# A sparse graph-attention layer on one core: another order of the tiles, two products added on VectorE, an earlier request and another queue for the records

## The chip, the cores and the metric

The kernel runs on one core of a Trainium2 chip. A core has a matrix engine (TensorE, PE in the profile, with its weight loads shown apart as PEld), a vector engine (VectorE, DVE), a scalar engine (ScalarE, ACT), a general engine (GpSimd, POOL) and a sync engine (SyncE, SP) that only issues transfers. Each engine works through its own list of instructions in order and waits on semaphores for the others; DMA queues are fed from SP, ACT and POOL. The metric is the device time of one execution in microseconds, and the median of several executions is compared.

## The reference, cut to what matters

There are 4096 source nodes `x` and 4096 target nodes `h_target`, each of width 512, and an adjacency matrix of 4096 x 4096 integers with about 17 nonzero entries in a row. Eight heads have 64 columns each.

```python
hs = layer_norm(x, ln1);  ht = layer_norm(h_target, ln1)
q = (ht @ Wq + bq) / sqrt(64);  k = hs @ Wk + bk;  v = hs @ Wv + bv
logits = where(adj != 0, q @ k.T per head, -1e30)
ctx = softmax(logits) @ v
h = layer_norm(ht + ctx @ Wo + bo, ln2)
out = layernorm(x + h + gelu(h @ W1) @ W2)
```

W1 is 512 x 2048 and W2 is 2048 x 512. Everything is in 32-bit floats.

## The kernel before, in words

The kernel uses the sparsity. It makes, for every target row, a list of its neighbours, and gathers only those rows of k and v.

The first stage, to about 300 us, projects all sources to rows of k and v (a row of 1024 floats, kept in the DRAM tensor `kvd`), while the adjacency matrix is read in quarters of a row tile, and DVE takes the positions of the nonzero entries from them (`edges`). The targets are in two parts of 16 tiles of 128 rows. In each part the rows are sorted by their number of neighbours (`sort`), and a record is written for each row at its place in that order (`recs_d`): the number of neighbours, the row's index, its layer-norm factors and the first 24 neighbours. So each tile has rows of nearly equal degree and a fixed number of slots, `CAPS_A` for the first part and `CAPS_B` for the second: 39, 24, 23, 22, 20 and so on down to 11, and 38, 24, 23 and so on down to 12. The 603 slots in all are one gathered row of k and v for each of 128 targets. The lists of the first part and of five tiles of the second are made in the first stage, those of the rest beside the attention of the first part (`other_lists`).

In the second stage two streams are woven together at build time: attention over the tiles, and the feed-forward network over groups of tiles. `_order` puts the tiles in groups, almost always two, and so gives the order in which all of it runs. The function `_weave` merges the streams by due times: each generator yields a cost, and the one that is furthest behind goes next. A group of two tiles counts 60 units in attention (`cost`, shared out by slots) and 60 in the feed-forward stream, whatever its number of slots. A scheduler then gives each engine its final list, so instructions of one engine can change places.

Attention takes the slots of a tile in groups of up to three (`S = 3`, list `SG`). For a group:

- POOL gathers its slots into the ring `kv` by indirect DMA (`issue`, `gather`, L964). The ring has 17 places for the first part and 20 for the second. `request` issues four groups ahead, or five.
- DVE multiplies k by q (L1197) and sums over each head (L1201); ACT takes the exponential (L1205, L1214).
- DVE multiplies v by the weights (L1161), except for the third slot of a full group, which ACT does head by head (`by_scalar`, L1178 and L1181).
- PE transposes the slots and adds them up in PSUM, four transposes a slot (L1169). In the second part DVE adds the products of the first two slots before (L1165), so that PE transposes one less:

```python
if m > 1 and i >= NA:
    nc.vector.tensor_add(kv[:, 0, D:], kv[:, 0, D:], kv[:, 1, D:])
    slots.remove(1)
```

Before a tile's first group, `prefetch` loads its record (L978), two tiles ahead, into one of seven buffers, and `front` makes its q. It gathers the rows of `h_target` (into `tq`, one of three buffers), scales them on ACT (L990), transposes them on PE (L994, copied back by ACT at L997), multiplies by Wq (L1003) and adds the bias on DVE (L1008). The steps of `front` are spread by `yield`; each is made when `advance` is called, twice for a group of slots. A tile with more than 24 slots gets the rest of its list from `rest_of`, by a gather from `rest_d` and four DVE instructions. `finish` divides by the sums, multiplies by Wo (L1096), adds the normalized target by transposing `tq` (L1092), and makes the second layer norm and its transposes (L1122). `feed` multiplies by W1 (L1304), takes the gelu on ACT (L1307), multiplies by W2 (L1313), gathers x, and `end` normalizes and scatters the rows to the output by indirect DMA on POOL (L1281). The record of a tile is used last by that scatter, so its buffer is free when the scatter has landed.

Of the kernel before, what the change touches and what calls it, by code (L numbers as in the profile page):

```python
# [17 lines left out]
P = 128  # L18
# [360 lines left out]
RW = E0 + RE  # L379
# [5 lines left out]
def _order():  # L385


    n, m = len(CAPS_A), len(CAPS_B)
    a = [(k * P, c) for k, c in enumerate(CAPS_A)]
    b = [((n + k) * P, c) for k, c in enumerate(CAPS_B)]  # L390
    groups = [[a.pop()]]
    while len(a) > 1:
        groups.append([a.pop(), a.pop()])
    groups.append(a + [b.pop()])
    while len(b) > 1:
        groups.append([b.pop(0), b.pop()])
    return groups + [b]


def _weave(*streams):  # L400
# [43 lines left out]
def adj_resnorm_kernel(  # L444
# [33 lines left out]
    nc = tc.nc  # L478
# [14 lines left out]
    SEGS = [(s * WS, min(s * WS + WS, WQ)) for s in range(SQ)]  # L493
    SEG = NQ * SQ
    groups = _order()
    TILES = [t for g in groups for t in g]
    GROUPS = []
# [3 lines left out]
    NA, NBT = len(CAPS_A), len(CAPS_B)  # L501
# [11 lines left out]
    recs_d = [dram.tile([n * P, RW], I32, name=f"rec{i}") for i, (_, n) in enumerate(PARTS)]  # L513
# [19 lines left out]
    with tc.tile_pool(name="keep", bufs=1) as keep:  # L533
# [17 lines left out]
        with ExitStack() as late:  # L551
# [19 lines left out]
                                                                       b=2, s=SEG)  # L571
# [196 lines left out]
            def rest_of(i):  # L768


                keep_rest()
                rec = recs[i]
                gid = lp.tile([P, 2 * SEG, 8], F32, name="gid")
                flat = gid.rearrange("p s e -> p (s e)")
                gather(flat, rest_d, rec[:, TGT:TGT + 1])
                yield
                for c in range(E0 + RE, E0 + MAXE, 8):
                    nc.vector.match_replace(flat, rec[:, c - 8:c], flat, 0.0)
                    nc.vector.max(rec[:, c:c + 8], flat)
                has = lp.tile([P, MAXE], F32, name="ehas")  # L780
                num = lp.tile([P, 1], F32, name="num")
                nc.vector.tensor_scalar(has, rec[:, E0:E0 + MAXE], 0.0, 0.0, op0=ALU.is_gt,
                                        op1=ALU.add, accum_out=num)
                part = 1 if TILES[i][0] >= PARTS[1][0] * P else 0
                nc.vector.tensor_tensor(bad[:, 6 + part:7 + part], num, rec[:, DEG:DEG + 1],
                                        ALU.not_equal)
# [174 lines left out]
            recs, tqs, h2Ts, done, ready = {}, {}, {}, set(), []  # L961

            def gather(dst, table, idx):
                nc.gpsimd.indirect_dma_start(  # L964
                    out=dst, out_offset=None, in_=table[:, :],
                    in_offset=bass.IndirectOffsetOnAxis(ap=idx, axis=0))

            def prefetch(i):
                if i >= NT or i in recs:
                    return  # L970
                r0 = TILES[i][0]
                part = 1 if r0 >= PARTS[1][0] * P else 0
                assert part in done
                r0 -= PARTS[part][0] * P
                rec = sp.tile([P, E0 + MAXE], I32, name="rec", bufs=7)

                eng = nc.gpsimd if i < 2 else nc.sync
                eng.dma_start(rec[:, :RW], recs_d[part][r0:r0 + P, :])  # L978
                recs[i] = rec

            def front(i):


                rec = recs[i]
                tq = sp.tile([P, 2 * D], F32, name="tq", bufs=3)
                t = tq[:, :D]
                gather(t, h_target, rec[:, TGT:TGT + 1])
                yield
                m = rec[:, RST:RST + 2].bitcast(F32)
                nc.scalar.activation(t, t, AF.Identity, bias=m[:, 1:2], scale=m[:, 0:1])  # L990
                yield
                pt = ps.tile([P, KC, P], F32, name="t", bufs=2)
                for kc in range(KC):
                    nc.tensor.transpose(pt[:, kc, :], t[:, kc * P:(kc + 1) * P], ident)  # L994
                hT = tq[:, D:].rearrange("p (c t) -> p c t", c=KC)
                for kc in range(KC):
                    nc.scalar.activation(hT[:, kc, :], pt[:, kc, :], AF.Identity,  # L997
                                         bias=b1r[:, kc:kc + 1], scale=s1c[:, kc:kc + 1])
                yield
                yield  # L1000
                pq = ps.tile([P, D], F32, name="t", bufs=2)
                for kc in range(KC):
                    nc.tensor.matmul(pq, hT[:, kc, :], wq[:, kc, :], start=kc == 0,  # L1003
                                     stop=kc == KC - 1)
                yield
                yield
                yield
                nc.vector.scalar_tensor_tensor(tq[:, :D], pq, HD ** -0.5, bqr,  # L1008
                                               op0=ALU.mult, op1=ALU.add)
                tqs[i] = tq  # L1010


            SG = [(i, j0, min(S, cap - j0)) for i, (_, cap) in enumerate(TILES)
                  for j0 in range(0, cap, S)]
            kvs, rests, fronts = {}, {}, {}
            place = [0]
            for i, _, n in SG:
                if place[-1] + n > RING[i >= NA]:
                    place[-1] = 0
                place.append(place[-1] + n)  # L1020
            first_b = next(k for k, (i, _, _) in enumerate(SG) if i >= NA)
            issued = [0]

            def step(gens, i):

                if i in gens and next(gens[i], StopIteration) is StopIteration:
                    del gens[i]

            def request(k):
# [3 lines left out]
                while issued[0] <= min(k + ahead, len(SG) - 1):  # L1033
# [3 lines left out]
                        assert not mine & set(range(place[m], place[m] + SG[m][2]))  # L1037
                    issued[0] += 1

            def issue(k):  # L1040

                i, j0, n = SG[k]
                if j0 == 0:
                    prefetch(i + 2)
                    if i not in tqs:
                        fronts[i] = front(i)
                        step(fronts, i)
                    if TILES[i][1] > RE:
                        rests[i] = rest_of(i)
                        next(rests[i])  # L1050
                elif j0 + n > 12 and i in rests:
                    for _ in rests.pop(i):
                        pass
                kvs[k] = ring[:, place[k]:place[k] + n, :]
                for j in range(n):
                    gather(kvs[k][:, j, :], kvd[0:N + 1, :], recs[i][:, E0 + j0 + j:E0 + j0 + j + 1])

            def finish(i, p, cps, group, hs, mv):


                rec, tq, cap = recs[i], tqs.pop(i), TILES[i][1]
# [33 lines left out]
                for c in range(KC):  # L1095
                    nc.tensor.matmul(pa, ct[:, c, :], wo[:, c, :], start=False,  # L1096
                                     stop=c == KC - 1, skip_group_check=True)
                yield
                h = sp.tile([P, D], F32, name="h")
                nc.scalar.copy(h, pa)  # L1100
# [33 lines left out]
            def first_fronts():  # L1134

                for i in range(EARLY):
                    prefetch(i)
                for i in range(EARLY):
                    fronts[i] = front(i)
                while fronts:  # L1140
                    go_on()
                    yield 4.0

            def attention():
# [10 lines left out]
                def values(i, j0, n, kv, p, cps, after):  # L1155

                    m = n - 1 if n == S else n
                    v4 = kv[:, :m, D:].rearrange("p j (h d) -> p j h d", h=H)  # L1160
                    nc.vector.tensor_tensor(v4, v4, p[:, j0:j0 + m, :].unsqueeze(3)  # L1161
                                            .to_broadcast([P, m, H, HD]), ALU.mult)
                    slots = list(range(n))
                    if m > 1 and i >= NA:
                        nc.vector.tensor_add(kv[:, 0, D:], kv[:, 0, D:], kv[:, 1, D:])  # L1165
                        slots.remove(1)
                    for j in slots:
                        for c in range(KC):
                            nc.tensor.matmul(cps[:, c, :], kv[:, j, D + c * P:D + (c + 1) * P], ident,  # L1169
                                             is_transpose=True, start=j0 + j == 0 and c == 0,  # L1170
                                             stop=j0 + n == TILES[i][1] and j == slots[-1],
                                             skip_group_check=True)
                    if after is not None:
                        tails.append(after)
# [10 lines left out]
                k = 0  # L1185
                for group in GROUPS:
# [3 lines left out]
                    for i in group:  # L1190
                        cps = ps.tile([P, KC, P], F32, name="cps", bufs=2)
                        while k < len(SG) and SG[k][0] == i:
                            _, j0, n = SG[k]
# [162 lines left out]
                for g in gens:  # L1356
                    yield from g

            EARLY = 2
            WAIT = 40.0  # L1360
            AHEAD = 4
            UNIT = 60.0
# [102 lines left out]
```

## Time and profile before

| | |
|---|---|
| median of 5 runs | 1865.05 us (1858.57 to 1867.39) |
| the profiled execution | 1856.79 us, its span 1855.0 us |
| PE, PEld busy | 1691.5 us, 1104.4 us |
| DVE busy | 1429.4 us |
| ACT busy | 1212.0 us |
| POOL busy | 960.9 us |
| kv gathers on POOL (L964) | 603, 750.4 us, 1244 ns each |
| transposes of slots (L1169) | 2008, 261.8 us |
| adds of two products (L1165) | 101, 68.6 us |
| end of the eighth tile, of the tile with 39 slots, of the last tile (L1066) | 604, 1026, 1710 us |

Busy time is the time in which an engine had an instruction in work; it is no measure of whether it set the pace. The windows give it for a stretch of the span, and the waits tell which engine or transfer an idle engine was waiting for. The times of the L1066 instruction, one for each tile, tell where attention is. In a line of the timeline the numbers are the start, the length, and in square brackets the idle time before it and what ended that. The compared times are of whole executions, and the profiled one lies 8 us below their median.

### The profile page before, as it was taken

The numbers are of one execution on the slowest core, as the hardware profiler recorded it, in microseconds if no ns is written. First come the engines' busy times: TensorE is split into PE (matmuls) and PEld (weight loads), VectorE is DVE, ScalarE is ACT, GpSimd is POOL, SyncE is SP. The second block draws the span as 40 slices with busy tenths as digits, with TensorE's granted clock in tenths as the row PEclk, the third lists the DMA queues.
The fourth block names the chain that finished last, engine by engine and source line by source line (L and its number), as shares of the span: only waits on it lengthen the run. The fifth ranks groups of instructions, "written<-read, shape, count | busy, mean of one in ns | idle before, by whom it ended". The sixth has DMA issues, their size and how long they took to land. (4 is left out here: it accounts for less than half of the span.)

```text
span 1855.0 us, 22978 instructions
## 1 busy us (share of the span) xinstructions
PE 1691.5 (91%) x7030; PEld 1104.4 (60%) x7030; DVE 1429.4 (77%) x2596; ACT 1212.0 (65%) x3111; POOL 960.9 (52%) x804
## 2 busy tenths in 40 slices
PE   7989974697989989999999989899999999999995
PEld 3434432475656656767666666576676666656663
DVE  6989855999989838777968999788978697778000
ACT  5767634587877637676767776676868676756211
POOL 1000143845646577657567788776657566643101
PEclk9999987799999989999999999899999999999998
DMA  9999959988877548768788888778777776763000
GB/s 353 364 378 375 346 168 353 337 289 315 295 274 235 201 137 301 260 227 273 252 275 301 266 301 285 245 263 264 222 251 241 247 261 222 248 204 114 23 0 25
DMA packets 147757, 463.28 MB, mean 250 GB/s; under 512 B 24468, under 2 KB 29160, under 8 KB 147624
## 3 DMA queue, kind: packets, MB, share of 16 engines
q0 software_dynamic: 95696, 342.19, 54.3%
q1 hardware_dynamic: 44112, 96.44, 14.7%
q10 hardware_dynamic: 7816, 23.08, 3.3%
q8 instruction: 58, 0.95, 0.2%
q14 instruction: 75, 0.61, 0.1%
HBM read 430.76 MB, written 30.89 MB: 249 GB/s over the span
## 5 line engine op out<-in xcount | busy, mean ns | idle before, releaser
L964 POOL DMA_INDIRECT kv<-kvd,rec x603 | 750.4, 1244 | 406.1 <-PE cps L1169 161.0
L1313 PE MATMUL po<-w,gt 128*128 128x512 f32 x1024 | 470.0, 602 | 7.2 <-ACT gt L1307 7.2
L1304 PE MATMUL pf<-h2T,w 128*128 128x256 f32 (+1 forms) x2176 | 472.2, 371 | 1.7 <-issue 1.7
L1197 DVE TENSOR_TENSOR kv<-kv,tq 128x1536 f32<-128x1536 f32 (+2 forms) x211 | 352.0, 1676 | 111.1 <-DMA kv<-kvd,rec 96.4
L1304 PEld LDWEIGHTS pf<-h2T,w 128*128 128x128 f32 x2176 | 393.9, 193 | 68.6 <-issue 23.4
L1181 ACT ACTIVATE kv<-kv,pa 128x64 f32<-128x64 f32 x1520 | 391.4, 336 | 4.5
L1201 DVE TENSOR_REDUCE lg<-kv 128x24 f32<-128x1536 f32 (+2 forms) x211 | 350.4, 1667 | 6.7 <-ACT pa L1178 5.7
L1313 PEld LDWEIGHTS po<-w,gt 128*128 128x128 f32 x1024 | 190.6, 194 | 205.2 <-issue 196.5
L1169 PEld LDWEIGHTS cps<-ident,kv 128*128 128x128 f32 x2008 | 237.9, 144 | 108.9 <-issue 49.0
L1169 PE MATMUL cps<-ident,kv 128*128 128x128 f32 x2008 | 261.8, 278 | 42.7 <-DVE kv L1161 39.6
L1161 DVE TENSOR_TENSOR kv<-kv,p 128x1024 f32<-128x1024 f32 (+1 forms) x211 | 250.8, 1193 | 19.2 <-ACT p L1205 9.7
L687 POOL TENSOR_TENSOR n_rs<-n_ve,mhalf 128x2 f32<-128x2 f32 (+2 forms) x51 | 54.2, 1063 | 349.7 <-DVE n_ve L680 144.6
L728 ACT ACTIVATE kv<-kv 128x1024 uint8<-128x1024 int32 x128 | 134.7, 1053 | 78.2 <-DMA kv<-in_adj_dram 40.0
L929 PE MATMUL pq<-wk,h2T 128*128 128x512 f32 x256 | 126.7, 639 | 11.8 <-ACT h2T L914 5.6
L1307 ACT ACTIVATE gt<-pf 128x512 f32<-128x512 f32 x128 | 76.3, 596 | 91.7 <-PE pf L1304 84.0
L735 DVE MAX8 cand<-kv 128x8 uint16<-128x103 uint16 (+1 forms) x640 | 130.4, 252 | 1.4 <-issue 0.5
L1307 ACT ACT_TABLE_LOAD x99 | 127.0, 1283 | 1.6
L1205 ACT ACTIVATE p<-lg 128x24 f32<-128x24 f32 (+2 forms) x179 | 39.0, 218 | 134.6 <-DVE lg L1201 100.2
L1003 PE MATMUL t<-wq,tq 128*128 128x512 f32 x256 | 118.6, 606 | 8.9 <-ACT tq L997 8.9
L929 PE MATMUL pq<-wv,h2T 128*128 128x512 f32 x256 | 115.3, 593 | 0.8 <-ACT tq L931 0.8
L1096 PE MATMUL t<-wo,rb 128*128 128x512 f32 x256 | 115.5, 592 | 0.0
L990 ACT ACTIVATE tq<-tq,rec 128x512 f32<-128x512 f32 x32 | 26.0, 813 | 110.0 <-DMA tq<-in_L_gnn_h_target_dram,rec 109.8
(156 smaller groups left out, 1574.3 us busy)
## 6 DMA issues: line engine op xcount, KB each, us to landing
kv<-in_adj_dram SPq DMA_DIRECT2D x128, 512.0 KB
kvd<-tq ACTq DMA_DIRECT2D x24, 512.0 KB
kv<-kvd,rec POOLq DMA_INDIRECT x603
kv<-in_L_gnn_h_target_dram SPq DMA_DIRECT2D x32, 256.0 KB
kv<-in_x_dram SPq DMA_DIRECT2D x15, 512.0 KB
rest_d<-gid SPq DMA_DIRECT2D x32, 160.0 KB
w<-in_L_gnn_W_dram SPq DMA_DIRECT2D x4, 1024.0 KB
kvd<-kv ACTq DMA_DIRECT2D x8, 512.0 KB
```

The costliest lines, as they stand in the source:

```text
L728: nc.scalar.activation(sg, a, AF.Sign, accum_out=dpart[:, i, h:h + 1])
L735: nc.vector.max(cand[:, h * SQ + s, :], wd[:, w0:w1])
L929: nc.tensor.matmul(pkv, hT[:, kc, j * P:(j + 1) * P], w[:, kc, :], start=kc == 0, stop=kc == KC - 1)
L964: nc.gpsimd.indirect_dma_start(out=dst, out_offset=None, in_=table[:, :], in_offset=bass.IndirectOffsetOnAxis(ap=idx, axis=0))
L1161: nc.vector.tensor_tensor(v4, v4, p[:, j0:j0 + m, :].unsqueeze(3) .to_broadcast([P, m, H, HD]), ALU.mult)
L1169: nc.tensor.matmul(cps[:, c, :], kv[:, j, D + c * P:D + (c + 1) * P], ident, is_transpose=True, start=j0 + j == 0 and c == 0, stop=j0 + n ...
L1181: nc.scalar.mul(v, v, pa[:, hd:hd + 1])
L1197: nc.vector.tensor_tensor(kv[:, :n, :D], kv[:, :n, :D], tq[:, :D].unsqueeze(1).to_broadcast([P, n, D]), ALU.mult)
L1201: nc.vector.tensor_reduce(lg[:, :n, :], kv[:, :n, :D].rearrange("p j (h d) -> p j h d", h=H), AX.X, ALU.add)
L1304: nc.tensor.matmul(pf[:, k, :], w1[(f0 + k) // KC][:, kc, (f0 + k) % KC * P:((f0 + k) % KC + 1) * P], h2T[:, kc, :w], start=kc == 0, stop= ...
L1307: nc.scalar.activation(gt, pf, AF.Gelu_apprx_tanh)
L1313: nc.tensor.matmul(po[j], gt[:, k, j * P:(j + 1) * P], w2[(f0 + k) // KC][:, (f0 + k) % KC, :], start=False, stop=f0 + k == FC - 1, skip_g ...
```

## The change

There are four edits. The first changes `_order`: the heaviest tile of each part, with 39 and 38 slots, moves from the border between the parts to a place inside its part, each with a partner of 13 slots as its own group. In slots the order of groups is

- before: 11; 13+14; 15+15; 16+17; 17+18; 19+19; 20+22; 23+24; 39+12; 38+13; 24+14; 23+15; 22+15; 20+16; 19+17; 18+17; 18
- after: 11; 14+15; 15+16; 17+17; 18+19; 19+20; 13+39; 22+23; 24+12; 24+14; 23+15; 22+15; 38+13; 20+16; 19+17; 18+17; 18

The second lets DVE add the products of two slots from the ninth tile on, instead of from the seventeenth. The third begins `front` of a tile up to two groups of slots sooner, when its `tq` buffer has been read by PE for the last time in program order (`turned`); its further steps are put off by as many calls, and by two more in the second part. The fourth issues all record loads from POOL, where the first two were, instead of from SP.

```diff
 def _order():
     groups = [[a.pop()]]
+    top = [a.pop(), a.pop(0)]
     while len(a) > 1:
         groups.append([a.pop(), a.pop()])
+    groups.insert(-1, top)
     groups.append(a + [b.pop()])
+    top = [b.pop(0), b.pop()]
+    rest = []
     while len(b) > 1:
-        groups.append([b.pop(0), b.pop()])
-    return groups + [b]
+        rest.append([b.pop(0), b.pop()])
+    rest.insert(len(rest) // 2, top)
+    return groups + rest + [b]
...
-                eng = nc.gpsimd if i < 2 else nc.sync
-                eng.dma_start(rec[:, :RW], recs_d[part][r0:r0 + P, :])
+                nc.gpsimd.dma_start(rec[:, :RW], recs_d[part][r0:r0 + P, :])
...
-            def front(i):
+            def front(i, idle=0):
...
                 gather(t, h_target, rec[:, TGT:TGT + 1])
-                yield
+                for _ in range(1 + idle):
+                    yield
...
+            def begin(i, lead):
+                if i not in begun_fronts:
+                    begun_fronts.add(i)
+                    fronts[i] = front(i, 2 * lead + (2 if i > NA else 0))
+                    step(fronts, i)
+
             def issue(k):
+                for d in (1, 2):
+                    if k + d < len(SG) and SG[k + d][1] == 0 and SG[k + d][0] - 3 in turned:
+                        begin(SG[k + d][0], d)
                 i, j0, n = SG[k]
                 if j0 == 0:
                     prefetch(i + 2)
-                    if i not in tqs:
-                        fronts[i] = front(i)
-                        step(fronts, i)
+                    begin(i, 0)
...
                 for c in range(KC):
                     nc.tensor.matmul(pa, ct[:, c, :], wo[:, c, :], start=False,
                                      stop=c == KC - 1, skip_group_check=True)
+                turned.add(i)
...
-                    if m > 1 and i >= NA:
+                    if m > 1 and i >= NA - 8:
```

More of the change, by code (lines that the diff above doesn't have):

```diff
@@ L1010, in front @@
                 tqs[i] = tq
+            EARLY = 2
             SG = [(i, j0, min(S, cap - j0)) for i, (_, cap) in enumerate(TILES)
@@ L1020, in adj_resnorm_kernel @@
                 place.append(place[-1] + n)
+            begun_fronts, turned = set(range(EARLY)), set()
             first_b = next(k for k, (i, _, _) in enumerate(SG) if i >= NA)
@@ L1357, in chain @@
                     yield from g
-            EARLY = 2
             WAIT = 40.0
```

## The prediction, made before the changed kernel was run

> **What bounds the kernel now.** I read the page's busy shares and slices first, then windows cut at the ends of tiles, then groups of instructions, waits, and single stretches of the timeline.
>
> ```profile
> PE 1691.5 (91%) x7030; PEld 1104.4 (60%) x7030; DVE 1429.4 (77%) x2596; ACT 1212.0 (65%) x3111; POOL 960.9 (52%) x804
> ...
> PE   7989974697989989999999989899999999999995
> ...
> DVE  6989855999989838777968999788978697778000
> ```
>
> The second of these, the slices, matters more than the shares: from slice 16 (about 720 us) on PE is full almost everywhere and stays so to the end, 130 us after DVE has nothing left to do. In slices 8 to 13 it is DVE that is full.
>
> ```profile
> 350.00:600.00 250.00, 217.06 (x1016) 151.01 (x1015) 233.58 (x508) 193.46 (x491) 140.79 (x109) 0.94 0.81 281
> ...
> 600.00:720.00 120.00, 111.73 (x492) 75.58 (x491) 78.14 (x98) 66.96 (x181) 79.21 (x69) 0.96 0.61 204
> 720.00:1026.00 306.00, 298.31 (x1405) 211.25 (x1404) 249.05 (x242) 226.70 (x635) 199.04 (x171) 0.98 0.78 266
> 1026.00:1160.00 134.00, 125.76 (x567) 87.77 (x566) 125.55 (x131) 97.08 (x278) 106.68 (x78) 0.97 0.84 283
> 1160.00:1700.00 540.00, 519.25 (x2199) 350.24 (x2198) 443.74 (x474) 384.23 (x1039) 342.78 (x276) 0.98 0.72 238
> 1710.00:1838.00 128.00, 124.71 (x524) 83.10 (x522) 12.71 (x74) 23.99 (x46) 10.25 (x12) 1.00 0.05 15
> ```
>
> Columns after the length: busy PE, PEld, DVE, ACT, POOL. Four regimes: 350 to 600, DVE at 93% with the list work of part two beside attention; 720 to 1026, PE at 97% and DVE at 81%; 1026 to 1160, the tiles of 12, 38 and 13 slots, DVE and PE both at 94%; then PE at 96% and DVE at 82%. So 94% is the highest share that DVE reaches here in a mixed stretch, and PE work that goes between 604 and 1700 is worth its own time as long as DVE stays below that.
>
> ```profile
> POOL kv L964 <- PE cps L1169: 161.0, 86, 15.7
> ...
> ACT tq L990 <- DMA tq<-in_L_gnn_h_target_dram,rec: 109.8, 25, 10.7
> ...
> DVE kv L1197 <- DMA kv<-kvd,rec: 96.4, 34, 12.4
> ```
>
> POOL waits for PE to free the ring: PE is what the others wait for. ACT's wait for h is long, but of it only the L994 transposes (20.9 us, four times) reach PE.
>
> ```profile
> 497.73 1.53 PE L1169 MATMUL cps<-ident,kv 128*128 128x128 f32 x12 [1.05 <-DVE kv L1161]
> ...
> 1255.66 1.75 DVE L1197 TENSOR_TENSOR kv<-kv,tq 128x1536 f32<-128x1536 f32 x1
> 1257.33 0.68 DVE L1165 TENSOR_TENSOR kv<-kv 128x512 f32<-128x512 f32 x1
> 1257.93 1.74 DVE L1201 TENSOR_REDUCE lg<-kv 128x24 f32<-128x1536 f32 x1
> 1259.59 1.21 DVE L1161 TENSOR_TENSOR kv<-kv,p 128x1024 f32<-128x1024 f32 x1
> 1260.72 1.75 DVE L1197 TENSOR_TENSOR kv<-kv,tq 128x1536 f32<-128x1536 f32 x1
> ...
> 757.95 0.99 POOL L1281 DMA_INDIRECT out_dram<-xt,rec  x1 [0.30 <-ACT rb L1073]
> 761.86 0.98 POOL L964 DMA_INDIRECT xt<-in_x_dram,rec  x1 [2.92 <-DMA out_dram<-xt,rec]
> ...
> 265.13 1.17 POOL L978 DMA_DIRECT2D rec<-rec  x2 [1.77 <-issue]
> 271.53 1.01 POOL L964 DMA_INDIRECT tq<-in_L_gnn_h_target_dram,rec  x1 [5.24 <-DMA rec<-rec]
> ```
>
> Prices: twelve transposes in 1.53 us, the last taking 0.28, so one costs (1.53 - 0.28) / 11 = 0.114 us. On DVE, start to start, a group of three slots costs 1.67 (L1197) + 1.66 (L1201) + 1.13 (L1161) = 4.46 us, 1.49 a slot; the add L1165 makes it 5.06. A record load on POOL takes 0.6 us plus 0.3 of issue, and what needs it at once waits 5.24 us more; a gather behind an output scatter waits 2.9.
>
> **What the Trainium skill says.** "Perfetto Trace Analysis", Identifying the Most-Contended Engine, warns that matmul busy time is no measure of distance to roofline. Agreed, PEld is only 69% busy from 720 to 1026; I take PE as the bound because of who waits for whom. "SBUF — State Buffer", Practical consequences, says that a DVE instruction with two SBUF inputs contends with a GpSimd one that reads SBUF. The kv gathers of POOL take 0.94 us or about 2 us and 1.24 in the mean, which fits; 59 more adds of that kind can cost POOL up to 59 x 0.6 = 35 us, against 161 us that it waits for PE. "DMA: Bandwidth & Descriptors", Anatomy of one DMA — SWDGE, gives 2.0 us plus bytes/436e3, an estimate of 2.0 us for a 14.5 KB record load; the trace has 5.24 after issue, and that is used.
>
> **The change part by part.**
>
> *Adds.* They now apply to tiles 8 to 15: 19, 19, 20, 13, 39, 22, 23 and 24 slots, in which 59 groups have two or more DVE slots. PE loses 59 x 4 = 236 transposes: 236 x 0.114 = **-27 us**, all after 600 us, where PE is the bound. DVE gains 59 x 0.60 = 35 us. Does it fit? Tiles 8 to 15 ran from 604 to 1026 with PE 111.7 + 298.3 = 410 and DVE 78.1 + 249.0 = 327 us busy. Five slots leave this stretch (123 instead of 118 lie in the first eight tiles): PE 410 - 27 - 2 = 381, DVE 327 + 35 - 7 = 355. On average DVE is 93% of PE, so mostly hidden.
>
> *Order, first half.* Not on average but in one pair it does not fit: 13 + 39 slots on DVE is 17 x 5.06 + 1.8 + about 12 (the other instructions of two tiles, and the 39 slots' own list end) = 100 us, at 94% 106; PE has some 94 to 97 (a pair of feeds, projections and transposes about 78, slots 52 x 0.456 - 7.8). **+10 us** there, 0 if DVE's lead of a few groups covers it, +20 if the stalls also cost clock. Five slots moved in front of 604 us meet a full DVE: 5 x 1.49 = **+7**, and **-2** of PE after it.
>
> *Order, second half.* Before, 39 + 12 and 38 + 13 slots stand back to back, and PE idles 7.7 us (720 to 1026) and 8.2 us (1026 to 1160). With 24 + 12 after the first, and 38 + 13 in the midst of part two behind pairs that leave DVE 18% free, I take half of the 16 back: **-8** (0 to -16). Moved with the 39-slot tile go its 39 kv gathers, its h gather, its gather of list rests and its record load; all stay in POOL's order, the latter three now in one run behind two scatters.
>
> *h sooner.* In the changed program as built, POOL's order has the h gather about 4 to 5 slots before its tile in part two, instead of about 2; but ACT's order has the scaling L990 at five groups before the tile instead of three or four. The consumer moves as far as the request. I take **0** (-15 if the L994 waits go, +10 if ACT waits longer). Behind a waiting L990 stand the exponentials, the by-ACT products and the gelus; PE waits for those.
>
> *Record loads.* 30 leave SP, where they waited 907 us that cost nobody (only at 497 us did list loads stand behind one), and enter POOL: 30 x 0.9 = 27 us, against POOL's 161 + 62 us of waiting for the ring. They stand right behind the scatters whose landing they wait for, where the x gather waited already, and seven h gathers follow their own record with at most one gather between: up to 7 x 5 = 35 us of POOL standing still, with kv gathers behind. DVE sees it when its ring of five to six groups runs dry. **+5 us** taken, 0 to +40.
>
> Sum: -27 - 2 + 7 + 10 - 8 + 0 + 5 = **-15 us**. The profiled execution took 1856.8 us with a span of 1855.0, so 1841.8 and a span of 1840; it is 8 us below the median of the five runs, so I forecast 1865 - 15 = **1850 us**.
>
> **Rivals.**
>
> A, *the uneven pair is absorbed and the h waits go*. DVE enters the heavy pair with its ring full, PE's idle 16 us come back, and half of the L994 and L1079 waits of PE go (20.9 + 24.0, half 22, of which some 5 lie in those 16 already): -27 - 2 + 7 - 16 - 17 = -55, so 1810. For: the 97% of PE ahead of the pair. Against: the L990 order above.
>
> B, *DVE becomes the bound in tiles 8 to 15* (slower). DVE was idle 426 - 327 = 99 us in this stretch, and waits for kv, ACT and POOL rather than merely for PE. If that idle time is not squeezed, the stretch takes 355 + 99 = 454 instead of 426: +28, with +7 and -8 that is +27: 1892 us; half squeezed, 1867. It decides from the point where idle stays above 71 us. Against: idle was 6% in 1026 to 1160.
>
> C, *POOL's run at the end of each feed starves DVE*. Scatter, landing, record, landing, h, and only then kv: some 4 us more at a dozen places, half of it passed on, +24: 1865 - 20 + 24 = 1869.
>
> D, *nothing moves*: the adds are paid where PE's time is saved. 1865.
>
> **How the numbers follow.** Forecast 0.50 (own range 1838 to 1862), A 0.17, B 0.16, C 0.09, D 0.08. A measurement of this kernel can tell about 0.3%, 5.6 us, from no change. Faster: 0.50 x 0.9 + 0.17 + a little of C = 0.63; slower: most of B and C and the tail of the forecast, 0.23; the same 0.14. Leaving half of A's tail and the upper part of B out, the range is 1820 to 1877.
>
> **What would show it.** L1169 with 1772 matmuls and L1165 with 160; the stretch from 604 us to the end of the 24-slot tile shorter by 15 to 25 us, with DVE near 90% and PE still above 94%; PE waiting for DVE (cps on L1161 or L1165) by about 10 us in the 13 + 39 pair; the h waits of ACT about as long as before; the POOL wait on record landings new, 10 to 35 us, and DVE's wait for kv up by less than 30. It is wrong if DVE's share there stays near 81% and the stretch does not shorten (B), or if PE's waits on L994 vanish and the time falls below 1835 (A).

## The result, and the profile after

| | before | after |
|---|---|---|
| median | 1861.4 us (79 runs, 1846.65 to 1875.39) | 1855.52 us (42 runs, 1846.13 to 1861.33) |
| ratio of the times, with 95% interval | 1 | 0.9971 (0.9962 to 0.9980) |
| profiled execution, its span | 1856.79 us, 1855.0 us | 1854.99 us, 1853.2 us |
| start of the last output scatter | 1838.8 us | 1844.7 us |
| from that start to the end of the span | 16.2 us | 8.5 us |

The change saves 0.29% or about 6 us, where 15 us were forecast. The last two rows hold the surprise. In the profiled executions all of the work ends 6 us later than before; the gain lies behind the last scatter, where nothing is computed any more. The profiled execution of the kernel before was 4.6 us faster than its median, so between the medians the work ends about 2 us later.

From the page of the changed kernel, the busy shares, the slices of PE and DVE, and the groups of the transposes and of the adds:

```profile
PE 1672.7 (90%) x6794; PEld 1080.7 (58%) x6794; DVE 1459.8 (79%) x2655; ACT 1229.3 (66%) x3125; POOL 974.0 (53%) x834
...
PE   7989974597999789989899899998989999999997
...
DVE  6989854899899767889898787887889897988200
...
L1187 PE MATMUL cps<-ident,kv 128*128 128x128 f32 x1772 | 243.1, 283 | 69.7 <-DMA kv<-kvd,rec 24.8
...
L1183 DVE TENSOR_TENSOR kv<-kv 128x512 f32<-128x512 f32 x160 | 109.2, 683 | 0.5
```

236 transposes are gone and 59 adds have come, as worked out: PE is busy 19 us less, DVE 30 us more. But in slices 15 to 22 (counted from 0, about 695 to 1065 us), where PE had nines alone, there are now three eights. The windows, cut at the ends of the eighth tile (628 us), of the 24-slot tile (1029), of the 12-slot tile (1054) and of the last tile (1719), have busy PE, PEld, DVE, ACT and POOL after the length. The first is of the kernel before, from its eighth tile to the end of its 39-slot tile; the others are of the changed kernel:

```profile
604.00:1026.00 422.00, 406.05 (x1874) 283.25 (x1873) 323.19 (x327) 291.08 (x809) 274.90 (x237) 0.98 0.73 248
```

```profile
628.00:1029.00 401.00, 364.31 (x1555) 247.37 (x1554) 339.50 (x366) 283.58 (x771) 284.54 (x237) 0.96 0.76 250
...
1054.00:1719.00 665.00, 641.74 (x2743) 432.46 (x2742) 555.36 (x597) 487.54 (x1302) 424.67 (x357) 0.99 0.72 242
```

The stretch that got the adds has PE at 364.31 / 401 = 91% and DVE at 339.50 / 401 = 85%. Before, the same eight places in the order had PE at 406.05 / 422 = 96% and DVE at 77%. So PE's saved time has partly become PE's idle time, and DVE is not full either. After 1054 us PE is at 96.5%, much as before. The first number behind the five busy times is the share of PE's full clock that was granted: 0.98 before and 0.96 after in this stretch. The waits name what PE waits for (us in total, times, longest):

```profile
POOL kv L970 <- PE cps L1187: 137.0, 68, 11.6
...
ACT tq L996 <- DMA tq<-in_L_gnn_h_target_dram,rec: 121.7, 27, 10.7
...
DVE kv L1215 <- DMA kv<-kvd,rec: 32.1, 10, 12.3
...
PE cps L1187 <- DVE kv L1183: 23.8, 9, 10.1
...
POOL rec L983 <- DMA out_dram<-xt,rec: 22.2, 9, 4.5
...
PE t L1000 <- ACT tq L996: 16.0, 3, 9.0
```

The line of PE and the add (L1187 and L1183) is new: 23.8 us of PE's waits end with the add, and the list before had no such entry. POOL waits less for PE (137.0 us, before 161.0), DVE much less for its gathers (32.1, before 96.4), and POOL now 22.2 us for scatters to land before a record load. ACT's waits for h are a little longer, and PE's at the h transposes a little shorter (16.0, before 20.9). One of the nine cases, in DVE's and PE's lines of the timeline:

```profile
786.28 1.23 DVE L1179 TENSOR_TENSOR kv<-kv,p 128x1024 f32<-128x1024 f32 x1 [4.19 <-ACT p L1232]
791.68 1.76 DVE L1215 TENSOR_TENSOR kv<-kv,tq 128x1536 f32<-128x1536 f32 x1 [4.18 <-DMA kv<-kvd,rec]
793.36 0.68 DVE L1183 TENSOR_TENSOR kv<-kv 128x512 f32<-128x512 f32 x1
...
794.10 1.97 PE L1187 MATMUL cps<-ident,kv 128*128 128x128 f32 x8 [5.16 <-DVE kv L1183]
```

The products are ready at 787.5 us. The add needs nothing else, but on DVE's list the multiply of the next group (L1215) stands ahead of it, and that waits 4.18 us for its gather. DVE idles with the add ready behind it, and PE, out of other work since 788.9 us, waits 5.16 us; without the add it could have started on the products at once. Not every case is so pure. Eight of the nine waits, 22.0 us, lie in tiles 8 to 15, and only some 12 us of these passed after the product was ready; in the other 10 us the product itself was late. In the longest one, 10.1 us, the product was ready 2.3 us before PE began. Of the 160 adds only 19 directly follow their product on DVE; 41 have a multiply L1215 of another group between, and 47 a reduce L1219 (counted in the trace; the rest has other work between, or more than one instruction).

Last, the instructions of POOL's end-of-program line (shortest, median and longest of three drains in ns), first in the kernel before:

```profile
L1460 POOLq DRAIN  x3: 44/107/8158, 1846.1 to 1854.8; - x3
```

and in the changed kernel:

```profile
L1477 POOLq DRAIN  x3: 44/107/1952, 1850.4 to 1852.9; - x3
```

One drain of POOL takes 8.16 us before and 1.95 us after. That is 6.2 of the 7.7 us by which the end came closer to the last scatter.

### The profile page after: what moved, and what is told of

Read it like the earlier page. It is cut to its first block, busy times and chain, and to the rows that moved or that the text cites. A ratio compares the mean times of both kernels' runs of the same rounds, so it can differ in the third digit from the quotient of the medians.

```text
span 1853.2 us, 22478 instructions
## 1 busy us (share of the span) xinstructions
PE 1672.7 (90%) x6794; PEld 1080.7 (58%) x6794; DVE 1459.8 (79%) x2655; ACT 1229.3 (66%) x3125; POOL 974.0 (53%) x834
## 5 line engine op out<-in xcount | busy, mean ns | idle before, releaser
L970 POOL DMA_INDIRECT kv<-kvd,rec x603 | 750.1, 1244 | 409.1 <-PE cps L1187 137.0
L1331 PE MATMUL po<-w,gt 128*128 128x512 f32 x1024 | 464.4, 596 | 2.7 <-ACT gt L1325 2.5
L1215 DVE TENSOR_TENSOR kv<-kv,tq 128x1536 f32<-128x1536 f32 (+2 forms) x211 | 351.8, 1676 | 36.3 <-DMA kv<-kvd,rec 32.1
L1219 DVE TENSOR_REDUCE lg<-kv 128x24 f32<-128x1536 f32 (+2 forms) x211 | 350.3, 1667 | 0.2
L1187 PE MATMUL cps<-ident,kv 128*128 128x128 f32 x1772 | 243.1, 283 | 69.7 <-DMA kv<-kvd,rec 24.8
L1187 PEld LDWEIGHTS cps<-ident,kv 128*128 128x128 f32 x1772 | 215.9, 147 | 142.0 <-issue 50.4
L734 ACT ACTIVATE kv<-kv 128x1024 uint8<-128x1024 int32 x128 | 134.8, 1054 | 85.9 <-DMA kv<-in_adj_dram 50.6
L935 PE MATMUL pq<-wk,h2T 128*128 128x512 f32 x256 | 122.5, 622 | 8.9 <-ACT tq L937 5.8
L935 PE MATMUL pq<-wv,h2T 128*128 128x512 f32 x256 | 119.2, 610 | 7.0 <-ACT kv L937 6.7
L1183 DVE TENSOR_TENSOR kv<-kv 128x512 f32<-128x512 f32 x160 | 109.2, 683 | 0.5
```

The lines of the kernel that those rows point to most:

```text
L734: nc.scalar.activation(sg, a, AF.Sign, accum_out=dpart[:, i, h:h + 1])
L935: nc.tensor.matmul(pkv, hT[:, kc, j * P:(j + 1) * P], w[:, kc, :], start=kc == 0, stop=kc == KC - 1)
L970: nc.gpsimd.indirect_dma_start(out=dst, out_offset=None, in_=table[:, :], in_offset=bass.IndirectOffsetOnAxis(ap=idx, axis=0))
L1215: nc.vector.tensor_tensor(kv[:, :n, :D], kv[:, :n, :D], tq[:, :D].unsqueeze(1).to_broadcast([P, n, D]), ALU.mult)
L1219: nc.vector.tensor_reduce(lg[:, :n, :], kv[:, :n, :D].rearrange("p j (h d) -> p j h d", h=H), AX.X, ALU.add)
L1331: nc.tensor.matmul(po[j], gt[:, k, j * P:(j + 1) * P], w2[(f0 + k) // KC][:, (f0 + k) % KC, :], start=False, stop=f0 + k == FC - 1, skip_g ...
```

## The experiments

Each ratio is to the kernel before on the same chip, in five rounds, with its 95% interval; the groups of experiments ran on different chips. Line numbers shift a little between kernels; the operations are named. "Tail" is the time from the start of the last scatter to the end of the span. The expectations number their theories. Mine at first was 1 (the adds pay, the new order takes part of it back) with 4 (the effects add up); against it stood 2 (DVE is the bound), 3 (h or the records take it back), 5 and 7 (the adds pay only with the early h, or with it and the order) and 6 (PE waits for the add). Later ones are on the records and the drain (8 to 11), on why the adds return nothing (12: DVE has no time; 13: PE waits for the add itself) and on h (15: the distance from gather to scaling; 16: q is ready sooner).

### One edit alone, and three without one

Eight kernels: each edit alone on the kernel before, and each undone in the changed kernel. The switches are

```diff
# adds                                     # records
-  if m > 1 and i >= NA:                   -  eng = nc.gpsimd if i < 2 else nc.sync
+  if m > 1 and i >= NA - 8:               +  eng = nc.gpsimd
# order: the body of _order                # h: front's idle steps, begin, turned
```

> The kernel before with the second edit alone: DVE adds two products from the ninth tile on (here the tiles of 18, 19, 19, 20, 22, 23, 24 and 39 slots). Theory 1 (adds pay, the new order eats it): 10 to 25 us faster than before, 236 to 248 transposes fewer. Theory 2 (DVE becomes the bound in these tiles): within 5 us of before or slower, DVE over 94% busy there. Theory 3 (adds pay, the h request or the record loads eat it): 10 to 25 us faster, like theory 1.

> The kernel before with the first edit alone: the new order of tiles. Theory 1: 5 to 15 us slower (five more slots in front of the ninth tile, where DVE is full, and nothing regained in part two). Theory 2: 5 to 10 us faster, since the heavy pairs are apart. Theory 3: within 5 us of before.

> The kernel before with the third edit alone: h requested sooner. Theory 1 and 2: within 4 us of before, since the scaling on ACT moves with the request. Theory 3: 5 to 12 us slower, PE waiting longer before the q matmuls (L1009) for ACT.

> The kernel before with the fourth edit alone: all record loads in POOL's queue. Theory 1 and 2: within 4 us of before. Theory 3: 5 to 10 us slower, POOL waiting for landings of scatters and records at the end of each feed.

> The changed kernel without the second edit (adds from the seventeenth tile on, as before). Theory 4 (the effects add up; alone they were order +0.14%, adds +0.43%, h -0.65%, records +0.55%): 0.7% faster than before. Theory 5 (the adds pay only where the h request is early and the 39-slot tile stands apart from the 38-slot one): between 0.3% slower and 0.2% faster, so slower than the changed kernel.

> The changed kernel without the first edit (order of tiles as before). Theory 4: 0.4% faster than before. Theory 5: 0.2 to 0.8% slower, the adds making DVE the bound around the adjacent tiles of 39 and 38 slots.

> The changed kernel without the third edit (h requested as before). Theory 4: 0.35% slower than before. Theory 5: 0.5 to 1% slower, since the record loads on POOL delay the h gather, and PE waits for the scaling, at every tile.

> The changed kernel without the fourth edit (records on SP, as before). Theory 4: 0.85% faster than before, and so 0.55% faster than the changed kernel. Theory 5: 0.3 to 0.6% faster than before, the record loads on POOL costing less when h is requested early.

| edit | alone | undone in the changed kernel (0.9971) | so worth there |
|---|---|---|---|
| adds | 1.0043 (1.0026 to 1.0060) | 1.0011 (0.9996 to 1.0025) | -0.40% |
| order | 1.0014 (0.9996 to 1.0031) | 0.9977 (0.9958 to 0.9995) | -0.06% |
| h sooner | 0.9935 (0.9911 to 0.9959) | 0.9996 (0.9981 to 1.0012) | -0.25% |
| records on POOL | 1.0055 (1.0038 to 1.0073) | 0.9956 (0.9938 to 0.9973) | +0.15% |

The edit that was priced at nothing, h, is the only one that gains alone: 12 us. The adds, meant to carry the forecast with -27 us, cost 8 us alone. The records cost 10 us alone and 3 us in the changed kernel. The order is worth nothing that these intervals can tell from zero. Theories 1 and 3 expected the adds to gain alone, and no theory expected a gain from h. Theory 2 has the sign of the adds, but not its reason: DVE was busy for 83% of their stretch and not for over 94%. Theory 3 has the records. With the edits undone, adds and records came out as theory 5 had it, the order nearest to theory 4, and h as neither.

The effects do not add up: alone they sum to +0.47%, together they make -0.29%. In the changed kernel the adds do gain, 0.40%. There the records are loaded from POOL; with them on SP, and the new order and the early h in both, the adds gain nothing (0.9956 with them, 0.9947 without, the latter from the next section). Put the other way, the records on POOL cost 0.64% without the adds and 0.15% with them. Why the two go together is not shown.

The profile of the kernel with the adds alone has the wait on the add, too:

```profile
PE cps L1169 <- DVE kv L1165: 27.9, 14, 5.5
```

### Two edits

The adds or the order on top of the earlier h, to see whether they need it.

> The kernel before with the second and third edits: DVE adds from the ninth tile on, and h requested sooner. Theory 6 (the adds return nothing anywhere: PE waits for the add, L1165, about as long as the transposes would have taken; they looked good in the changed kernel only against its record loads): 0.5 to 0.9% faster than before, like the h edit alone at 0.65%. Theory 7 (the adds need the early h and bring their 25 us then): 1.2 to 1.8% faster.

> The kernel before with the first and third edits: new order and early h. Theory 6: 0.4 to 0.7% faster than before, the order being worth about nothing. Theory 7: 0.1% slower to 0.2% faster: without the adds the new order is only a load, as in the changed kernel without the adds (+0.11%).

Adds with h: 0.9950 (0.9933 to 0.9968); order with h: 0.9947 (0.9931 to 0.9962). Either is within 0.15% of h alone (0.9935), so the adds return nothing even there: theory 6 for both, and theory 7 is refuted. In the profile of adds with h PE's wait for the add is larger still. Of these 35.3 us, 22 lie in tiles 8 to 15, as with the adds alone (21) and in the changed kernel (22); the rest is of the second part:

```profile
PE cps L1182 <- DVE kv L1178: 35.3, 16, 5.7
```

### The cost and the gain of the adds, each alone

On top of the earlier h, two kernels for tiles 8 to 15. In the first, DVE makes the adds but writes them into the used-up k half of the slot, and PE transposes all slots as before: the cost without the gain. In the second, the second slot is neither added nor transposed: the gain without the cost.

```diff
 # cost alone
+    elif m > 1 and i >= NA - 8:
+        nc.vector.tensor_add(kv[:, 0, :D], kv[:, 0, D:], kv[:, 1, D:])
 # gain alone
+    elif m > 1 and i >= NA - 8:
+        slots.remove(1)
```

> The kernel before with the third edit, and in the ninth to sixteenth tile DVE adds the two products as in the second edit, but writes the sum over the used k of the first slot; PE still transposes every slot. So the adds are paid and nothing is saved. Theory 12 (capacity: DVE's own time comes back as PE's wait): 15 to 30 us slower than with the h edit alone, so 0.2 to 0.9% slower than before. Theory 13 (PE loses only because its transposes now wait for the add itself): at most 5 us slower than with the h edit alone, 0.4 to 0.65% faster than before.

> The kernel before with the third edit, and in the ninth to sixteenth tile the second slot of a group is neither added nor transposed: its product is left out of the sum. So PE's saving comes without DVE's cost. Theory 12: 15 to 27 us faster than with the h edit alone, 1.4 to 2.1% faster than before. Theory 14 (PE's time is not worth its length even there, since DVE, POOL and ACT hold the tiles up): less than 8 us faster than the h edit alone.

Cost alone: 0.9894 (0.9865 to 0.9923), not slower than h alone, as theory 13 had it. Gain alone: 0.9825 (0.9797 to 0.9852), some 20 us below h alone; so theory 14 is out, and PE's time is worth most of its length. The following table is worked out from the traces, for the stretch from the end of the eighth to that of the sixteenth tile. "Need" is PE's instructions at the shortest spacing seen for their width, 109, 215 and 429 ns for 128, 256 and 512 columns, and "lost" is the rest. "Idle" is the part of it in gaps of over 0.15 us, and the last column is the time in which PE was granted half of its clock.

| kernel, with h | stretch | PE need | PE lost | of it idle | idle until the add | at half clock |
|---|---|---|---|---|---|---|
| no adds here | 424 us | 398 | 26 | 17 | none | 14 |
| cost alone | 427 us | 400 | 28 | 18 | none | 14 |
| gain alone | 406 us | 375 | 32 | 22 | none | 17 |
| both | 434 us | 386 | 49 | 30 | 22 | 31 |

With both, the need falls by 12 us and not by 23 as with the gain alone, since more of the feed-forward work lies in the stretch; what counts is the time lost. It grows by 23 us: 13 are more idle time, and the other 10 go with PE's clock, at half for 31 us instead of 14. In the trace four of the five stretches at half clock begin in, or just behind, a wait of over 2 us for the add. So the waits seem to bring the lower clock; no run tests that by itself. Of the 22 us, some 16 passed after the product was ready. The table is of single executions, and the profiled one of the cost-alone kernel was the slowest of five, 13 us over their median; the four ratios carry the argument.

DVE's time for the adds is free, and PE's saving is worth most of its 27 us, if PE need not wait for the add. Both together give nothing: what they have and neither half has is that PE's transposes hang on the add, which DVE reaches late. The profile of the cost-alone kernel, where DVE makes as many adds but PE doesn't need those of tiles 8 to 15, shows for the same entry (what is left is of the second part):

```profile
PE cps L1184 <- DVE kv L1178: 6.3, 5, 4.0
```

A kernel in which each add directly follows its product on DVE's list was not run, so that this order alone would return the 20 us is inferred.

### h requested as early, without the delay of the later steps

```diff
-    fronts[i] = front(i, 2 * lead + (2 if i > NA else 0))
+    fronts[i] = front(i)
```

> The kernel before with the third edit but without its delay: the gather of h and all the steps behind it begin up to two groups sooner. Theory 15 (what pays is that the scaling on ACT no longer comes before the landing, so the distance from gather to scaling): most of the gain goes, 0.1% slower to 0.3% faster than before. Theory 16 (what pays is that q is ready sooner): as fast as the third edit or faster, 0.55 to 0.8%.

1.0452 (1.0420 to 1.0485): some 96 us slower than h with the delay, and 84 slower than before. Theory 16 is refuted, and theory 15 missed the size by far. Waits on the way of h, first in the kernel before, then with h alone, then without the delay:

```profile
PE t L994 <- ACT tq L990: 20.9, 4, 8.6
```

```profile
ACT tq L991 <- DMA tq<-in_L_gnn_h_target_dram,rec: 105.0, 23, 11.6
...
DVE kv L1210 <- DMA kv<-kvd,rec: 58.9, 25, 12.5
...
PE t L1004 <- ACT tq L998: 9.1, 4, 3.5
...
PE t L995 <- ACT tq L991: 7.1, 2, 5.7
```

```profile
DVE kv L1210 <- DMA kv<-kvd,rec: 221.4, 75, 13.9
...
ACT tq L991 <- DMA tq<-in_L_gnn_h_target_dram,rec: 79.5, 25, 7.3
...
PE t L995 <- ACT tq L991: 39.0, 10, 10.4
...
PE t L1135 <- ACT h L1126: 19.6, 9, 5.1
...
PE t L1004 <- ACT tq L998: 17.0, 8, 5.1
```

Medians over tiles 18 to 32, from the traces:

| | before | h | h without the delay |
|---|---|---|---|
| gather of h ahead of the tile's first kv gather on POOL's list | 2 slots | 4 | 3 |
| from the gather of h to its scaling on ACT | 4.9 us | 4.9 us | 4.6 us |
| from the end of the scaling to the transposes on PE | 12.5 us | 23.3 us | 2.6 us |

In all three ACT scales h about as soon as it has landed, so the distance from gather to scaling, which theory 15 names, is not what differs. What the early request lengthens is the room between the scaling and PE's transposes. PE's wait there falls from 20.9 to 7.1 us, and all of its waits together from 143 to 131 us, about the 12 us gained. Without the delay PE comes to the transposes 2.6 us after the scaling, and its waits add up to 200 us. This is read from the traces; the delay moves all later steps of `front` at once, and no run moves the transposes alone.

It explains the 96 us only in part. PE also waits longer for the output of the second layer norm (h, L1126), and DVE's wait for its gathers rises from 58.9 to 221.4 us, while ACT waits less for h than before. POOL waits for PE to free the ring, DVE for POOL, ACT for DVE and PE for ACT; where in this circle the loss begins was not taken apart.

### The records: their landing waits, and the drain

First, the buffer of the record was made free before the scatter, by keeping the row's index in a small tile, so that the record load has no scatter to wait for.

```diff
+    nc.vector.tensor_copy(tgts[:, i:i + 1], recs[i][:, TGT:TGT + 1])
...
-    ap=recs[i][:, TGT:TGT + 1], axis=0),
+    ap=tgts[:, i:i + 1], axis=0),
```

> The changed kernel, with the row index of a tile copied by DVE into a small tile of its own when x is gathered, so that the last scatter of a tile reads the copy and the record's buffer is free half a feed earlier: the record load waits for no scatter's landing any more (the degrees go into a part of the tile that the last check uses anyway). Theory 10 (the record loads cost by that wait on POOL): 0.3 to 0.6% faster than the changed kernel, 0.6 to 0.9% faster than before. Theory 11 (they cost by what they take of POOL and by the lists that the scheduler makes with them): within 0.2% of the changed kernel.

0.9998 (0.9978 to 1.0018), no gain over 0.9971. That alone doesn't refute theory 10, since the edit only moved the wait: the record loads no longer stand behind a scatter, and now the gathers of x do, for 28.3 us. In the changed kernel it is 22.2 us at the record loads and 4.1 at x; in the kernel before it was 22.3 at x. So POOL waits about as long for its scatters whether it loads the records or not, and what the records cost lies elsewhere. Then the drain of POOL, with which the program ends. 30 small loads on POOL, which nobody needs, were added to the kernel before, in its first stage; and to the earlier h, 10, 30 and 60 of them after the last gathers, into the ring (the cut shows the first of these kernels):

```diff
+    for j in range(30):
+        nc.gpsimd.dma_start(pad[j:j + 1, :], h_target[j:j + 1, 0:16])
```

> The kernel before with 30 small loads more in POOL's queue in the first stage (16 floats each, into a tile that nothing reads). In the five profiles whose records are loaded by POOL the span ends 8.5 us after the issue of the last scatter, in the five others 16.1 us. Theory 8 (the number of DMAs that POOL has issued decides how long its last drain takes): the end shortens to some 8.5 us, and the kernel is 0.3 to 0.4% faster. Theory 9 (it is the emptier SP queue, or the place of the record loads): the end stays at 16 us and the time within 0.15% of before.

> The kernel before with the third edit (early h), and 30 small loads in POOL's queue when the gathers are done, into ring places that are no longer read. Theory 8 (the count of POOL's DMAs shortens its last drain): 1.0 to 1.15% faster than before, the end 6 to 9 us after the last scatter instead of 16, and faster than any other kernel here. Theory 9 (place or SP queue): 0.65% faster, like the h edit alone, or a little less.

> The earlier request for h, with 10 instead of 30 small loads on POOL's queue after the last gathers (their data lands in an unused part of the ring). Theory 8 (the length of the last drain on POOL falls with the number of transfers that POOL has issued through its queue): a time between that of the earlier request alone (0.9935) and that with 30 loads (0.9878), some 0.991, and a stretch of 10 to 14 us from the last scatter to the end. A threshold instead of a slope: 16 us or 5.5 us, and 0.9935 or 0.988. If the 30 loads work by something else than their count (their place late in the queue), 10 at the same place do as well as 30: 5.5 us.

> The same with 60 loads. Theory 8 as a slope: nothing is left to save below the 5.5 us of 30 loads, so 0.988 and 5 us; if the drain depends on where the count stands in a ring of fixed length, it comes back in part: 8 to 16 us, and 0.990 to 0.995. If the loads cost POOL more than they save, slower than with 30 by up to 60 x 0.9 = 54 us less what lies beside other work: 0.99 to 1.01 with a short drain.

| kernel | ratio | tail | long drain |
|---|---|---|---|
| before + 30 loads early | 1.0001 (0.9973 to 1.0029) | 6.0 us | 0.72 us |
| h | 0.9935 (0.9911 to 0.9959) | 16.0 us | 8.16 us |
| h + 10 loads | 0.9927 (0.9903 to 0.9950) | 17.2 us | 8.97 us |
| h + 30 loads | 0.9878 (0.9850 to 0.9906) | 5.5 us | 0.72 us |
| h + 60 loads | 0.9902 (0.9872 to 0.9933) | 12.0 us | 3.32 us |

The drain's own lines for 10, 30 and 60 loads:

```profile
L1474 POOLq DRAIN  x3: 50/109/8972, 1831.6 to 1841.1; - x3
```

```profile
L1474 POOLq DRAIN  x3: 50/109/724, 1828.8 to 1830.1; - x3
```

```profile
L1474 POOLq DRAIN  x3: 50/109/3317, 1844.5 to 1848.3; - x3
```

Ten loads lengthen it by 0.81 us, 30 more after the thirtieth by 2.59, so 0.081 and 0.086 us a load; between 10 and 30 it falls by 8.25 us. Neither "more transfers, shorter drain" (theory 8) nor a threshold fits. A sawtooth does, as the last expectation had it for a ring of fixed length: the drain grows with each transfer of POOL and starts anew somewhere. Four counts do not prove it. The early loads cut the tail by 10 us as well and gained nothing, so what the drain saves was lost before it; in that profile the eighth tile ends at 614 us instead of 604. The tail is the same within 0.4 us in all profiles with the same transfers on POOL: 16.0 to 16.4 without the records and 8.4 to 8.7 with them. Everything up to the last scatter is less steady: the last tile of the kernels with 10, 30 and 60 loads ends at 1699, 1698 and 1711 us, though they differ only in the loads that POOL issues from 1678 us on. A body that differs by 13 us in single profiles is therefore no finding; the ratios are. The kernel with h and 30 loads, 1834.8 us in the median, has the lowest time of those that leave no part of the work out, and is faster than both; h with the adds' cost alone (0.9894) is within its interval.

## Why the prediction was wrong, step by step

- **Adds, -27 us, with +10 for the uneven pair.** Counts and prices were right: 1772 transposes, 160 adds, and the gain alone returned some 20 us. The step that failed is "On average DVE is 93% of PE, so mostly hidden". It asked whether DVE has the time, and DVE has: the cost alone is nothing. It did not ask when DVE reaches the add. A new dependence was laid from DVE's list to PE, and the list runs in order behind another group's multiply or reduce. The wait was forecast for the pair of 13 and 39 slots alone, at 10 us, and there it was 10.3; outside it was put at nothing and was 12 us more in tiles 8 to 15. With the order as before, where there is no such pair, the wait in these tiles is as long, 21 us with the adds alone and 22 with h. The term is +8 us alone, +3 with h (which the intervals cannot tell from nothing), -7 with the other three, where -17 was put. "+20 if the stalls also cost clock" was named and not taken; PE's granted clock did fall, to 0.96 from 0.98.
- **h sooner, 0.** Failed: taking nothing because "the consumer moves as far as the request". That is so for the scaling on ACT, 4.9 us behind the gather before and after. But PE is the bound, and its transposes did not move along: they had 23.3 us behind the scaling instead of 12.5. Alone h is -12 us, in the changed kernel -5. The bound given (-15 if the L994 waits go) held the value.
- **Record loads, +5.** The time that they cost was undersized, and a gain was not seen. Alone they cost 10 us in spite of a tail that is 7.6 us shorter, so up to the last scatter some 18; in the changed kernel 3 + 7.6, or about 10. The wait on landings was 22.2 us, in the stated 10 to 35, but it was no new wait: the x gathers had had it before. DVE's wait for kv, expected to grow by up to 30 us, grew to 112.1 with the records alone and fell in the changed kernel. What in the records costs the rest, POOL's own time or another order on its list, stays open. The tail was in no step: the chain of waits ends at the last scatter, and I took what follows as fixed.
- **Order, +7, -2, -8.** The sum, -3 with the pair left out, agrees with nothing measurable. The +7 looks undersized: the eighth tile ends at 628 us, 24 later, and with the order alone at 621. But the ratio with the order alone is neutral, so it must have come back later.
- **Sum.** Forecast -15; measured -6, of which the shorter tail is -7.7. So without it the four edits together give about +2, nothing. The direction was right by luck, through a term that was not in the sum.
- **Rivals.** D (the adds are paid where PE's time is saved) comes nearest: up to the last scatter nothing moved. B (DVE is the bound) read the stretch rightly, DVE at 85% and no shortening from 604 us (1029 against 1026), but the cost-alone kernel refutes its mechanism. Its "half squeezed, 1867" does not come out of its own numbers: half of the 99 us left idle gives 404.5 us, and so some 1842. A named the L994 waits, which h alone cuts to a third, but the waits at L1079 stayed (24.8 us with h alone) and the pair did wait. C has its sign with the records alone; its row of landings does not show, since POOL waits no longer for scatters than before. None named an add that PE waits for outside the pair.
- **The Trainium skill.** "SBUF — State Buffer", Practical consequences, led to a bound of 35 us on POOL's gathers. The page after has 603 gathers at 1244 ns, the same as before, so 59 more two-input DVE instructions did not slow them in the mean.

## What to carry to other kernels

When work is moved from the bounding engine to one with room, ask of the result where it stands in the new engine's list and what the instruction ahead of it waits for: busy shares say whether it fits, the list says when it comes. Test such a move by making its cost and its gain apart, each in a kernel of its own; here that took two runs and told what ten combinations of the edits had not. When a request is made earlier, ask which steps behind it move along and which do not. And read what lies behind the last useful instruction before a small gain is put down to the body.

## What the runs showed of the hardware

The drain of POOL at the end of the program takes between 0.72 and 8.97 us here, and changes with the transfers that POOL issued: from 735 (8.16 us) it rises with 10 more by 0.81, is 0.72 with 30 more, and 3.32 with 60 more. 30 record loads of 128 rows gave 1.95 us where 30 loads of one row gave 0.72, so the count of transfers alone does not fix it; bytes or rows may enter. It took 0.72 us wherever the 30 small loads stood, at the start or at the end. Where the period lies, if it is one, was not measured. In this kernel a difference of this kind, up to 8 us, can hide or feign the effect of an edit that adds or takes away transfers on POOL.
